# A graph network on one core: keep the rows' state in SBUF, fold the node work into the attention pass, and change the order of the blocks

## The chip, the core and the metric

The program runs on one core of one Trainium2 chip. The metric is the device time of one execution in microseconds, from three runs. The engines named below are PE (TensorE, matrix multiply; PEld is its weight load), DVE (VectorE), ACT (ScalarE), POOL (GpSimd, which here issues all gathers and scatters) and SP (SyncE, which here issues most plain DMAs).

## The reference, cut to what matters

There are 6250 nodes with 48 features and 200000 edges from `src` to `dst`; each edge has 40 attributes. Four graph layers follow each other. The first holds nearly everything that the change touches:

```python
h = _ln(h + agg / tot[:, None], gn, bn)          # agg, tot: gated sums over edges
logm = jnp.log(jnp.clip(node_mult, 1.0, None))
for i in range(4):
    Q = _ln(h @ Wq[i], gq[i], bq[i]);  K = _ln(h @ Wk[i], gk[i], bk[i])
    qi = Q[src];  kj = K[dst]
    score = (qi * kj).sum(-1) + 0.1 * (edge_attr * qi[:, :40]).sum(-1) + logm[dst]
    es = jnp.exp(jnp.minimum(score - segment_max(score, src)[src], 20.0))
    alpha = es / (segment_sum(es, src)[src] + 1e-10)
    aggi = segment_sum(alpha[:, None] * (h[dst] @ Wm[i]), src)
    z = jnp.concatenate([h, aggi], axis=-1) @ Wu[i]
    h = _ln(h + jnp.where(z > 0, z, 0.01 * z), go[i], bo[i])
```

The second layer is two plain neighbour sums, the third (`gated`) is a gated sum with a division by the same `tot`, the fourth is a normalised neighbour sum.

## The kernel before, in words

**Rows and blocks.** The nodes are padded to 6272, which is 49 blocks of 128. `build_grid` sorts the edges by source node into a grid: every node as a source gets a *row*, and the rows are ordered by how many edges do not fit the regular part. A row has 49 regular slots (one per block of destination nodes) and `WS[b]` overflow slots. `WS` falls from 28 in block 0 over 24, 17, 16, 15 and so on to 4 in block 48; it sums to 502. `grid.nat` holds, for every row, the node that it belongs to, so rows are in one order and nodes in another.

**first_sums** (line 1007) walks the 49 row blocks. It gathers each row's own element vector (`ei`, line 1060, from the table `tails`), picks destination rows from `table0` by one-hot matmuls (`pick_rows`), gathers those of the overflow slots one slot at a time (`tr_o`, line 1076), scatters lists for a later layer (line 1084), keeps the edge logit of the third layer in SBUF (`g.logit`), and scatters the block's sums by an indirect DMA into `agg0` in node order (`put_rows`, line 1197, called at the end of the block).

**node1** (line 1527) reads `agg0` back and normalises all 49 blocks at once.

**Four attention layers.** Each has three stages. The *qk* stage multiplies all nodes' `h` by Wq and Wk (`product`), normalises both (`norm`) with instructions over all 49 blocks, and writes `table_k` (K and h) and `table_q` to DRAM in node order (lines 1552 and 1553). `attend` (line 1205) first reads the whole `table_k` back and splits it into three bf16 parts (`load_table`, `exact_parts`, lines 981 to 990). Then, block after block in the order 0 to 48, it loads the one-hot rows `hot_t` and the attributes `at`, gathers the rows' queries (`q`, line 1222) and the overflow keys (`kh`, line 1225, one indirect DMA per overflow slot), picks the 49 regular slots by 147 matmuls (line 1002, copied out by ACT at line 1003), computes scores in three pieces (lines 1231 to 1233, the third piece being the overflow slots), the softmax (lines 1234 to 1240), a tree of adds (line 1193), and scatters the block's sum into `agg` (line 1199). The *up* stage (line 1556) reads `agg` back, multiplies by Wu, and updates `h`, again with instructions over all 49 blocks.

**gated_sums** (line 1251) has the same shape as `attend` with 48 wide rows and one product per slot; a later instruction multiplies its result by the reciprocal of `tot`.

**What sets the order.** Tiles of a pool rotate: `kh` in `attend` and `xe` in `gated_sums` have two buffers, so a block's gathers and its picks wait until the block two before it has been summed. A scheduler orders the instructions of each engine when the program is built; on the chip each engine then runs its list strictly in that order, and waits on semaphores. Gathers, scatters of sums and `q` share POOL's one list.

Of the kernel before, what the change touches and what calls it, by code (L numbers as in the profile page):

```python
# [18 lines left out]
F32 = mybir.dt.float32  # L19
BF = mybir.dt.bfloat16  # L20
# [479 lines left out]
T0 = H + 2 * G + 2  # L500

# [505 lines left out]
def first_sums(ctx: ExitStack, tc: tile.TileContext, g, keep, dram, table0, tails, agg):  # L1007
# [27 lines left out]
    g.logit = keep.tile([P, NB * NB + WO[NB]], F32, name="logit")  # L1035
# [18 lines left out]
    def overflow(b):  # L1054
# [4 lines left out]
        ei = sp.tile([P, 2 * G], F32, name="ei")  # L1059
# [52 lines left out]
    recs = load(0, spans, g.grid)  # L1112
    hrs = heads_to_rows(0, recs)
    others, ei = overflow(0)
    for b in range(NB):
        T = NB + WS[b]
        bs = g.bias[:, g.col[b] : g.col[b] + T]
# [4 lines left out]
        def add(t0, n, rec, tr):  # L1122
# [12 lines left out]
            nc.vector.tensor_mul(pr[:, :n], tr[:, :n, H : H + 2 * G], ei[:, None, :].to_broadcast([P, n, 2 * G]))  # L1135
# [3 lines left out]
            nc.vector.tensor_mul(g.logit[:, g.col[b] + t0 : g.col[b] + t0 + n], lg[:, :n, 1], rec[:, :, CW])  # L1139
# [23 lines left out]
        for i, (s0, n) in enumerate(spans):  # L1163
# [9 lines left out]
            if i == 1 and b + 1 < NB:  # L1173
                ahead = load(b + 1, spans, g.grid)
        if b + 1 < NB:
            hrs = heads_to_rows(b + 1, ahead)
# [3 lines left out]
        sm = sp.tile([P, H + 1], F32, name="sm")  # L1180
        add_up(nc, acc, PC, sm[:, :H])
        nc.vector.reduce_sum(sm[:, H:], ac[:, : len(done)].rearrange("p i o -> p o i"), AX.X)
        put_rows(tc, agg, g.nat, b, sm, "agg0")
        if b + 1 < NB:
            recs = ahead
            others, ei = overflow(b + 1)
# [18 lines left out]
def attend(ctx: ExitStack, tc: tile.TileContext, g, table_k, table_q, agg, name):  # L1205
# [3 lines left out]
    with tc.tile_pool(name=f"{name}_l", bufs=1) as lp:  # L1209
        parts = load_table(nc, lp, one, table_k, 2 * H, f"{name}_k")  # L1210
    sp = ctx.enter_context(tc.tile_pool(name=f"{name}_e", bufs=2))
    pp = ctx.enter_context(tc.tile_pool(name=f"{name}_ps", bufs=6, space=PSUM))
    TM = NB + WS[0]
    for b in range(NB):
        T, W = NB + WS[b], WS[b]
        hot = sp.tile([P, NQ // 4], I32, name="hot_t")
# [4 lines left out]
        q = sp.tile([P, H], F32, name="q")  # L1221
        nc.gpsimd.indirect_dma_start(out=q, out_offset=None, in_=table_q, in_offset=rows(g.nat, b))  # L1222
        kh = sp.tile([P, TM, 2 * H], F32, name="kh")
        for w in range(W):
            nc.gpsimd.indirect_dma_start(out=kh[:, NB + w], out_offset=None, in_=table_k,  # L1225
                                         in_offset=rows(g.idx, WO[b] + w))
# [466 lines left out]
```

## Time and profile before

The three runs took 15986.23 us in the median (15978.01 to 16000.76). The profiled execution took 15998.33 us by the device's time, and its span in the profile is 15996.5 us.

The span, cut by stage (busy us of each engine inside each window, all from the trace):

| stage | window, us | length | PE | DVE | ACT | POOL |
|---|---|---|---|---|---|---|
| build_grid and first nodes' work | 0 to 4488 | 4488 | 1922.83 | 2242.59 | 1277.35 | 2057.03 |
| first_sums | 4488 to 7237 | 2749 | 898.31 | 1321.60 | 1142.16 | 1185.58 |
| attend, layer 1 | 8683 to 9798 | 1115 | 484.62 | 803.64 | 257.48 | 778.36 |
| up 1 and qk 2 | 9798 to 9976 | 178 | 65.54 | 75.48 | 35.02 | 0.49 |
| attend, layer 2 | 9976 to 11105 | 1129 | 479.28 | 803.89 | 256.12 | 790.53 |
| up 2 and qk 3 | 11105 to 11283 | 178 | 65.54 | 75.48 | 35.25 | 0.54 |
| attend, layer 3 | 11283 to 12396 | 1113 | 474.63 | 803.52 | 256.19 | 780.06 |
| up 3 | 12396 to 12463 | 67 | 31.43 | 28.55 | 13.17 | 0.23 |
| second layer | 12463 to 14108 | 1645 | 719.28 | 348.14 | 172.66 | 987.98 |
| gated | 14108 to 15151 | 1043 | 285.46 | 476.05 | 117.07 | 711.47 |
| fourth layer | 15151 to 15996 | 845 | 340.05 | 203.31 | 74.97 | 495.98 |

To read it: an engine's busy time counts its instructions alone. POOL's list has a gap of about 0.30 us before each indirect DMA that the busy time leaves out. Where no engine is near the length of its window, the stage is a chain of waits; a wait is laid to the instruction that released it. The window of layer 0 and the stretches around it belong to the prediction below.

### The profile page before, as it was taken

Reading aid. Unit: us, or ns where it says so; the run is one execution under the profiler, and the core shown is the slowest. Engines: PE = TensorE matmul, PEld = TensorE weight load, DVE = VectorE, ACT = ScalarE, POOL = GpSimd, SP = SyncE. Lnnn points to the kernel's source line nnn. Section 1 sums busy time; section 2 is a strip of 40 time slices with the busy share of each in tenths; the row PEclk is TensorE's granted clock in tenths of the full one; section 3 lists DMA queues with packets and bytes.
Section 4 is the critical chain, followed back from the end, with each engine's and each line's share of the span. In section 5 each row is a group of like instructions: output and inputs, shape, how many; then the busy total and the mean of one; then the engine's idle time right before and its main releaser. Section 6 shows DMA issues by size and latency. Waiting matters only on the chain. (4 is left out here: it accounts for less than half of the span.)

```text
span 15996.5 us, 185891 instructions
## 1 busy us (share of the span) xinstructions
PE 6350.0 (40%) x69181; PEld 5257.0 (33%) x69181; DVE 8133.3 (51%) x15302; ACT 3955.4 (25%) x9383; POOL 8573.7 (54%) x7381
## 2 busy tenths in 40 slices
PE   1255444444412333332443444345344344532234
PEld 1234333333312222332343343344234333322233
DVE  8544444444424445554685686577578212134522
ACT  0133333333323344451222122122122101011100
POOL 0445555555444444433773773675577466666566
PEclk9955655556555556665665666666566566556566
DMA  8632222222145556663343343333334333233432
GB/s 299 202 117 85 54 57 55 56 55 56 49 137 166 183 190 209 216 232 82 108 128 76 105 125 88 96 116 95 97 112 123 66 67 69 66 90 116 119 79 57
DMA packets 1247387, 1798.32 MB, mean 112 GB/s; under 512 B 845706, under 2 KB 965998, under 8 KB 1188741
## 3 DMA queue, kind: packets, MB, share of 16 engines
q1 hardware_dynamic: 875810, 1059.45, 22.2%
q0 software_dynamic: 241632, 351.07, 10.2%
q10 hardware_dynamic: 129024, 375.81, 6.1%
q8 instruction: 543, 8.90, 0.2%
q14 instruction: 378, 3.10, 0.1%
HBM read 1220.28 MB, written 572.63 MB: 112 GB/s over the span
## 5 line engine op out<-in xcount | busy, mean ns | idle before, releaser
L1002 PEld LDWEIGHTS <-hot_t 128*128 128x128 fp8e4 x36015 | 2034.8, 117 | 3728.8 <-issue 3712.4
L1002 PE MATMUL pick_ps<-att_k_b,hot_t 128*128 128x96 bf16 x28812 | 1921.6, 242 | 2775.6 <-ACT kh L1003 1800.2
L1225 POOL DMA_INDIRECT kh<-table_k,idx_g x2008 | 2523.4, 1257 | 857.6 <-issue 547.8
L970 POOL DMA_INDIRECT grid<-rec,sloti x1666 | 1930.8, 1159 | 1863.8 <-DVE lf L684 1034.4
L1003 ACT COPY kh<-pick_ps 128x480 f32<-128x480 f32 (+1 forms) x1960 | 965.6, 568 | 3172.2 <-DVE sm L1195 1086.9
L1314 PE MATMUL h_ps<-x_parts,am 128*128 128x144 bf16 (+1 forms) x7203 | 856.6, 269 | 1185.8 <-issue 981.8
L1306 POOL DMA_INDIRECT xe<-table_c,lt x980 | 987.7, 1008 | 580.5 <-issue 277.3
L1231 DVE SCALAR_TENSOR_TENSOR kh<-at,kh 128x1000 f32<-128x1000 f32 (+9 forms) x588 | 575.1, 978 | 1167.2 <-DMA kh<-table_k,idx_g 437.7
L1314 PEld LDWEIGHTS <-am 128*128 128x128 fp8e4 x7203 | 632.4, 116 | 1384.5 <-issue 1380.6
L966 PE MATMUL pg<-w,hid 97*128 97x96 f32 x3332 | 693.1, 363 | 872.8 <-ACT hid L963 778.1
L966 PEld LDWEIGHTS pg<-w,hid 97*128 97x128 f32 x3332 | 603.6, 262 | 1144.9 <-ACT hid L963 886.3
L1311 DVE TENSOR_TENSOR h_hot<-ld,h_lanes 128x1280 bf16<-128x1280 bf16 x147 | 218.5, 1490 | 1348.0 <-remote 1109.8
L1002 PE MATMUL pick_ps<-table_b,hot_b 128*128 128x114 bf16 x7203 | 643.4, 257 | 573.4 <-issue 481.4
L900 ACT ACTIVATE junk<-dup_ps,less 128x128 bf16<-128x128 f32 x1666 | 588.7, 365 | 759.6 <-PE dup_ps L897 475.4
L1002 PEld LDWEIGHTS <-hot_b 128*128 128x128 bf16 x7203 | 549.8, 123 | 657.4 <-issue 657.1
L1222 POOL DMA_INDIRECT q<-table_q,nat x196 | 219.4, 1119 | 1004.1 <-DVE att_k_b L984 696.8
L967 DVE TENSOR_TENSOR rec<-pg,cut 128x384 f32<-128x384 f32 (+1 forms) x441 | 235.9, 535 | 996.7 <-remote 643.5
L1076 POOL DMA_INDIRECT tr_o<-table,idx_g x502 | 497.9, 992 | 421.7 <-DVE acc L1193 199.7
L1268 POOL DMA_INDIRECT xe<-table_g,idx_g x502 | 605.4, 1206 | 218.5 <-issue 145.7
L963 ACT ACTIVATE hid<-ph,w1b 96x512 f32<-96x512 f32 (+1 forms) x441 | 290.1, 658 | 1686.2 <-remote 1010.4
L1193 DVE TENSOR_TENSOR kh<-kh 128x96 f32<-128x96 f32 (+16 forms) x980 | 705.6, 720 | 0.4
L1168 PE MATMUL dt_ps<-f_identb,hot_b 128*128 128x128 bf16 x2401 | 279.5, 272 | 1011.2 <-DVE hot_b L1157 664.8
(408 smaller groups left out, 16014.9 us busy)
## 6 DMA issues: line engine op xcount, KB each, us to landing
hot_t<-hot SPq DMA_DIRECT2D x245, 784.0 KB
grid<-zero ACTq DMA_DIRECT2D x150, 1127.0 KB
recs<-grid SPq DMA_DIRECT2D x348, 483.0 KB
am<-adj SPq DMA_DIRECT2D x48, 2352.0 KB
hr<-heads_g SPq DMA_DIRECT2D x147, 448.0 KB
low<-lows SPq DMA_DIRECT2D x49, 1088.0 KB
gate_g<-g ACTq DMA_DIRECT2D x156, 336.0 KB
attr_g<-at ACTq DMA_DIRECT2D x156, 280.0 KB
```

Of the source, the lines that this page charges most:

```text
L900: nc.scalar.activation(junk, ps[:, t], AF.Sign, bias=less13[:, way : way + 1], accum_out=dup[:, t0 + t : t0 + t + 1])
L966: nc.tensor.matmul(pg[:, k], ht[:, k * P : (k + 1) * P], w2, start=True, stop=True)
L970: i = nc.gpsimd.indirect_dma_start(out=g.grid, out_offset=rows(sloti, t), in_=rec[:, t, :], in_offset=None, bounds_check=SLOTS - 1, oob_is ...
L1002: nc.tensor.matmul(ps[:, d], hot(db0 + d0 + d), parts[:, db0 + d0 + d, k], start=(k == 0), stop=(k == 2))
L1003: nc.scalar.copy(dst[:, d0 : d0 + m], ps[:, :m])
L1076: nc.gpsimd.indirect_dma_start(out=tr[:, w], out_offset=None, in_=table0, in_offset=rows(g.idx, WO[b] + w))
L1193: nc.vector.tensor_add(t[:, :k], t[:, :k], t[:, n - k : n])
L1225: nc.gpsimd.indirect_dma_start(out=kh[:, NB + w], out_offset=None, in_=table_k, in_offset=rows(g.idx, WO[b] + w))
L1231: nc.vector.scalar_tensor_tensor(k[:, :, :R], at[:, t0 : t0 + n], 0.1, k[:, :, :R], OP.mult, OP.add)
L1268: nc.gpsimd.indirect_dma_start(out=xe[:, NB + w], out_offset=None, in_=table, in_offset=rows(g.idx, WO[b] + w))
L1306: nc.gpsimd.indirect_dma_start(out=xe[:, t], out_offset=None, in_=table, in_offset=bass.IndirectOffsetOnAxis(ap=g.lt[:, d0 + d, t, 0:1], a ...
L1314: nc.tensor.matmul(ps[:, d], am[:, b, d * P : (d + 1) * P], parts[:, b].rearrange("p k f -> p (k f)"), start=(b == 0), stop=False)
```

## The change

The rows' state stays on chip in row order, and the node work is done in row order, seven blocks at a time.

- **Order of blocks.** All three row passes (`first_sums`, `attend`, `gated_sums`) visit the blocks as 0, 48, 1, 47, ..., 23, 25, 24 (`ORDER`), so that a block with many overflow slots alternates with one that has few. Position `pos` in this order is the index of all state kept on chip.
- **first_sums** gathers the row's own `h` along with `ei` (the rows of `tails` grow from 64 to 112 floats) and copies it to `h_rows`. It adds the block's sums straight into the SBUF tiles `agg0` and `tot_r`; the scatter of the sums is gone. The third layer's logit goes to DRAM (one small DMA per block from ACT's queue) instead of staying in SBUF.
- **node1 and the first qk** run over seven groups of seven positions. The normalisation (`scaled`) now takes its inverse square root by a shift and three Newton steps on DVE, where `norm` used ACT's square root.
- **attend** reads its query from SBUF (`q[:, pos]`) and has no gather of `q`. It writes its sum into `cat`, and after every seventh position calls `update`, which does for these seven blocks what *up* and the next layer's *qk* did for all: transposes, products, normalisations, then seven `put_rows` scatters into the next layer's `table_k`. `table_q` and `agg` are gone. The copies out of PSUM of these products move from DVE to ACT.
- **load of the table** goes through seven chunks of seven blocks, each split into parts as it arrives; the pool for `pick_ps` has 5 buffers where it had 6.
- **The last layer** scatters `h` to `h_nodes` and reads it back; `x` is read here and not before the four layers.
- **gated_sums** loads the logit, and multiplies the sum by the row's `tot_r` itself.

```diff
+ORDER = [b for i in range(NB // 2) for b in (i, NB - 1 - i)] + [NB // 2]
+GN = 7
...
-    g.logit = keep.tile([P, NB * NB + WO[NB]], F32, name="logit")
+    g.logit = dram.tile([NB, P, NB + OS], F32, name="logit")
...
-        ei = sp.tile([P, 2 * G], F32, name="ei")
+        ei = sp.tile([P, 2 * G + H], F32, name="ei")
...
-    for b in range(NB):
+    for pos, b in enumerate(ORDER):
+        after = ORDER[pos + 1] if pos + 1 < NB else None
         T = NB + WS[b]
+        nc.scalar.copy(h[:, pos], ei[:, 2 * G :])
+        lgt = sp.tile([P, NB + OS], F32, name="lgt")
...
-        sm = sp.tile([P, H + 1], F32, name="sm")
-        add_up(nc, acc, PC, sm[:, :H])
-        nc.vector.reduce_sum(sm[:, H:], ac[:, : len(done)].rearrange("p i o -> p o i"), AX.X)
-        put_rows(tc, agg, g.nat, b, sm, "agg0")
+        nc.scalar.dma_start(g.logit[b, :, :T], lgt[:, :T])
+        add_up(nc, acc, PC, agg[:, pos])
+        nc.vector.reduce_sum(tot[:, pos : pos + 1], ac[:, : len(done)].rearrange("p i o -> p o i"), AX.X)
...
-def attend(ctx: ExitStack, tc: tile.TileContext, g, table_k, table_q, agg, name):
+def attend(ctx: ExitStack, tc: tile.TileContext, g, table, q, name, update):
...
-    pp = ctx.enter_context(tc.tile_pool(name=f"{name}_ps", bufs=6, space=PSUM))
+    pp = ctx.enter_context(tc.tile_pool(name=f"{name}_ps", bufs=5, space=PSUM))
+    npp = ctx.enter_context(tc.tile_pool(name=f"{name}_nps", bufs=1, space=PSUM))
+    parts = one.tile([P, NB, 3, 2 * H], BF, name="k_parts")
+    rows_of = table.rearrange("(b p) f -> p b f", p=P)
+    for d0, n in chunks(NB, 7):
+        t = sp.tile([P, 7, 2 * H], F32, name="k_f")
+        nc.sync.dma_start(t[:, :n], rows_of[:, d0 : d0 + n])
+        exact_parts(nc, t[:, :n], [parts[:, d0 : d0 + n, k] for k in range(3)])
...
-        nc.gpsimd.indirect_dma_start(out=q, out_offset=None, in_=table_q, in_offset=rows(g.nat, b))
...
-            nc.vector.tensor_mul(k, k, q[:, None, :].to_broadcast([P, n, H]))
+            nc.vector.tensor_mul(k, k, q[:, pos : pos + 1].to_broadcast([P, n, H]))
...
-        nc.vector.tensor_scalar(sm, sm, den, None, OP.mult)
-        put_rows(tc, agg, g.nat, b, sm, f"{name}_agg")
+        nc.vector.tensor_scalar(cat[:, pos % GN, H:], sm, den, None, OP.mult)
+        if pos % GN == GN - 1 or pos == NB - 1:
+            update(np_, npp, pos // GN * GN, pos % GN + 1, cat)
...
+        lg = sp.tile([P, TM], F32, name="lg")
+        nc.sync.dma_start(lg[:, :T], g.logit[b, :, :T])
...
+    def scaled(np_, src, k):
...
+        yi = y.bitcast(I32)
+        nc.vector.tensor_scalar(yi, v.bitcast(I32), 1, None, OP.logical_shift_right)
+        nc.vector.tensor_scalar(yi, yi, -1.0, float(0x5F3759DF), OP.mult, OP.add)
+        nc.vector.tensor_scalar(v, v, -0.5, None, OP.mult)
+        for _ in range(3):
+            nc.vector.tensor_mul(s, y, y)
+            nc.vector.tensor_mul(s, s, v)
+            nc.vector.scalar_tensor_tensor(y, s, 1.5, y, OP.add, OP.mult)
+        nc.vector.tensor_mul(xc, xc, wide(y, H))
...
+    def ask(np_, pp, l, p0, n, table, q):
+        v = hr[:, p0 : p0 + n]
+        qk = np_.tile([P, n, 2 * H], F32, name=f"qk{n}")
...
+        times(np_, pp, v, H, n, wqk[:, l].rearrange("k t m -> k (t m)"), 2 * H, put)
+        xc = scaled(np_, qk.rearrange("p n (t f) -> p (n t) f", t=2), 2 * n).rearrange("p (n t) f -> p n t f", t=2)
+        nc.vector.tensor_mul(xc, xc, gqk[:, l : l + 1].to_broadcast([P, n, 2, H]))
+        nc.vector.tensor_add(q[:, p0 : p0 + n], xc[:, :, 0], each(bqk[:, l, 0], n))
+        kh = np_.tile([P, n, 2 * H], F32, name=f"khn{n}", bufs=2)
+        nc.vector.tensor_add(kh[:, :, :H], xc[:, :, 1], each(bqk[:, l, 1], n))
+        nc.scalar.copy(kh[:, :, H:], v)
+        for i in range(n):
+            put_rows(tc, table, grid.nat, ORDER[p0 + i], kh[:, i], f"table_k{l}")
...
+        def update(np_, pp, p0, n, cat):
+            v = hr[:, p0 : p0 + n]
+            nc.scalar.copy(cat[:, :n, :H], v)
+            zs = np_.tile([P, n, H], F32, name=f"zs{n}")
...
+            times(np_, pp, cat, 2 * H, n, wc[:, l], H, put)
             nc.vector.scalar_tensor_tensor(zs, zs, 0.01, zs, OP.mult, OP.max)
-            nc.vector.tensor_add(zs, zs, h)
-            norm(np_, h, zs, NB, each(go[:, l]), each(bo[:, l]))
+            nc.vector.tensor_add(zs, zs, v)
+            xc = scaled(np_, zs, n)
+            nc.vector.tensor_mul(xc, xc, each(go[:, l], n))
+            nc.vector.tensor_add(v, xc, each(bo[:, l], n))
+            if l + 1 < L:
+                ask(np_, pp, l + 1, p0, n, tables[l + 1], qs[(l + 1) % 2])
+            else:
+                for i in range(n):
+                    put_rows(tc, h_nodes, grid.nat, ORDER[p0 + i], hr[:, p0 + i], "h_nodes")
```

## The prediction

> **What bounds the kernel now.** I read first the busy shares, then the busy time by stage, then who waited for whom inside one attention pass, then the stretch between two passes in order of time.
>
> ```profile
> span 15996.5 us, 185891 instructions
> ...
> PE 6350.0 (40%) x69181; PEld 5257.0 (33%) x69181; DVE 8133.3 (51%) x15302; ACT 3955.4 (25%) x9383; POOL 8573.7 (54%) x7381
> ```
>
> No engine is near full over the whole span, so the answer lies in the stages. Columns below: window, its length, busy us (instructions) of each engine, granted clock, DMA share, GB/s. The windows are node1 with the first qk, the start and the rest of the first pass, and one stretch between passes:
>
> ```profile
> 7237.00:7386.00 149.00, 34.39 (x149) 28.34 (x148) 71.85 (x44) 26.16 (x23) 0.00 (x0) 0.50 0.24 50
> 7386.00:7500.00 114.00, 34.94 (x504) 29.47 (x505) 39.64 (x40) 17.74 (x35) 62.07 (x58) 0.59 0.47 106
> 7500.00:8505.00 1005.00, 448.17 (x6704) 416.82 (x6700) 764.12 (x1039) 238.66 (x555) 723.42 (x543) 0.65 0.40 114
> 8505.00:8683.00 178.00, 65.54 (x294) 57.48 (x294) 75.49 (x54) 35.39 (x37) 0.00 (x0) 0.50 0.19 41
> ```
>
> The reader is to see two kinds of stage. **Between passes** POOL does nothing and DVE is busy 75 of 178 us: a chain. **Inside a pass** DVE is busy 76%, POOL 72%, plus 0.30 us before each of its 543 DMAs (163 us): 886 of 1005. The waits inside the pass:
>
> ```profile
> DVE kh L1231 <- DMA kh<-table_k,idx_g: 103.3, 15, 16.6
> DVE kh L1231 <- DMA q<-table_q,nat: 80.7, 15, 10.6
> DVE kh L1231 <- issue: 29.1, 10, 8.6
> ...
> POOL kh L1225 <- ACT kh L1003: 62.9, 34, 3.7
> ```
>
> DVE lacks gathered rows for 184 us (the first two rows; the wait laid to `q` is the same wait for POOL's list), POOL lacks free buffers. Both are nearly full in turn. The chain between passes, in order of time:
>
> ```profile
> 8502.39 0.98 POOL L1199 DMA_INDIRECT agg<-sm,nat  x1 [7.80 <-DVE sm L1245]
> ...
> 8504.92 0.68 SPq L1559 DMA_DIRECT2D cat<-agg  x1
> ...
> 8641.23 0.37 SPq L1552 DMA_DIRECT2D table_k<-kh  x1
> 8652.01 0.68 SPq L990 DMA_DIRECT2D att_k_f<-table_k  x1
> ...
> 8683.18 0.99 POOL L1222 DMA_INDIRECT q<-table_q,nat  x1 [179.81 <-DVE att_k_b L984]
> ```
>
> From the last sum (8502) to the next pass's first gather (8683) pass 181 us: a re-read of 8.5, products, three normalisations with 2.61 us instructions over 2352 elements, a table write of 11 and a re-read of 12, then 19 of `exact_parts` one after another.
>
> **The change part by part.** I work against the span, 15996.5.
>
> *Stretch between passes, three times.* What remains on the path is the last group of seven blocks. Products: the same code took 5.5 us for two chunks (8513.4 to 8518.9), and 7 for the wider qk product (7272.9 to 7279.9). Vector work: 336-element instructions cost 0.49 (the 0.47 to 0.50 of line 1193's), 672-element ones 0.85, tiny ones 0.24 when each depends on the last (lines 1234, 1236, 1237 start 0.24 apart). Update: 8 x 0.49 + 14 x 0.24 + about 1 for ACT's square = 8. Ask: 5 x 0.85 + 2 x 0.49 + 14 x 0.24 + 1 = 10. Then seven scatters at 1.25 (0.95 + 0.30) and 2.5 to land (8502.39 to the release at 8504.85): 11. With handovers: 5.5 + 8 + 7 + 10 + 11 + 3 = **45**. The re-read in chunks (12 us of DMA, then parts of 0.6 to 0.8 us each) runs beside the first block's 28 gathers (35 us), which have no parts to wait for. So 181 becomes 45: **-408** in all. If that cover is gone, up to 20 per stretch come back.
>
> *node1 with the first qk.* The agg0 re-read (10) goes. Seven groups at 10 x 0.49 + 5 x 0.85 + 28 tiny at 0.16 (two groups interleave) = 13.6 of DVE make 95; a start at 7238, when the weights are in, and 21 for filling and the last scatters end at 7354 instead of 7386: **-30**.
>
> *End of the last layer.* 69 us from the last sum to the next normalisation become 5.5 + 8 + 11 + 11 (re-read) + 3 + 3: **-28**.
>
> *Order of blocks.* I cut the passes of before into pairs of neighbours and put time against their mean overflow count W: attend 30.8 us at W = 5, 42 to 45 at 10, 48.3 at 12, 54.7 at 14; first_sums 82, 110, 122, 138. Nearly straight lines, so mixing heavy with light gains little by itself. Reading each new pair off these points: attend's 47 later blocks 1016 us instead of 1002 (the two taken out of the list are now 28 and 4, not 28 and 24), and the first pair 87 instead of 114, since only 4 gathers follow the 28: **-13** per pass. gated is less straight (26 at W = 5, 42.5 at 10, 50 at 14, cheap light blocks lost): **+42**. first_sums: 0.
>
> *Inside the pass, POOL.* 49 gathers of `q` and 49 scatters of `agg` go, 49 scatters of the table come, all elsewhere in POOL's list (the built program puts the seven scatters three to four blocks after their update, so POOL doesn't stand at them). Per DMA 1.24 + 0.30: **-76** of POOL's list per pass at most; nothing, if DVE ends each pair.
>
> Here a rule speaks against the change: the Trainium skill (DMA: Bandwidth & Descriptors, "Rules for kernel authors") says to join small transfers, since under 64 KB one pays mostly overhead. One table write of 2.4 MB becomes 49 of 49 KB; by that page's fit (2.0 us plus bytes over 436e3, Anatomy of one DMA) 49 x 2.1 = 103 us, an estimate. The row is nearer: POOL is held 1.54 each, 76 us, and only the last seven end on the path. I take the row.
>
> *Inside the pass, DVE.* Each update adds 13.6 to 16, seven make 100 per pass (45 in the last, which has no ask). In the built program's list these instructions stand one by one between those of the next blocks, so their handovers to PE and ACT have cover, and some fill the 184 us of waits for gathers. Bounds: all hidden, 0; none, +100. I take half, **+50**.
>
> A second rule: the Trainium skill (GPSIMD Engine Reference, "Specifications") says that POOL's SBUF port is shared with VectorE, and that VectorE instructions with two SBUF inputs contend. The trace shows it in gated:
>
> ```profile
> 14652.05 3.10 DVE L1271 TENSOR_TENSOR gt<-gt,logit 128x2832 f32<-128x2832 f32 x1
> 14652.14 4.05 POOL L1199 DMA_INDIRECT agg_g<-sm,nat  x1 [7.58 <-DVE xe L1193]
> ...
> 14664.76 0.95 POOL L1268 DMA_INDIRECT xe<-table_g,idx_g  x1 [0.30 <-issue]
> ```
>
> By the rule taken whole, the two-input part of an update (60 of 100 us) would stop POOL for 60. By the rows, attend's 600 DMAs last 0.30 longer than 0.95 on average: 180 us of delay for 804 of DVE, so 100 more cost POOL 22. I take 22. Net of POOL: 76 - 22 = 54, of which some 60% count: -33, together with the DVE's +50 and the order's -13 about **+4**, less the last pass's missing ask and a shorter first wait; rounded, a pass goes from 1116 to **1095**: **-84** for four.
>
> *first_sums.* The scatter `agg` leaves POOL's list, where it stood behind the gathers' wait: 1.30 x 49 = 64; not every block is at POOL's mercy, so **-45** (ends -64 and 0). The logit's DMA (0.33 on ACT's queue) waits for the block's last logit; behind it stand copies that wait for the next loads anyway: 0, at worst 3 x 49. The tails' write of `h` goes out where SP stands idle for 90 us: 0.
>
> Sum: -408 - 30 - 28 - 84 + 42 - 45 = -553, less one 2.6 us product at the end: **15440** for the span. The median lies 10 below the span: **15430**.
>
> **The rivals.**
> - *Forecast: the serial stretches go, the pass stays as long.* 15200 to 15680. Chance 0.56.
> - *Both engines pack.* With `q` gone and gathers evened out, DVE's 904 us end the pass with 70 for its start: 975 to 1040, so 14950 to 15210, say 15080. For it: light blocks of before ran DVE at 88% (356 of 405 us). Against it: straight lines above. 0.20.
> - *Update added in full.* POOL's gain is void, DVE's 100 us come on top: 87 + 1016 + 100 = 1203 per pass, +348 for four; -408 - 30 - 28 - 45 + 42 - 3 + 348 = -124: 15860 in the median. 0.18.
> - *Slower: PE starves under the gathers.* While POOL gathers without pause, PE gets an instruction only every 1.4 us:
>
> ```profile
> 7441.64 0.24 PE L1002 MATMUL pick_ps<-att_k_b,hot_t 128*128 128x96 bf16 x1 [2.56 <-issue]
> ```
>
> An update and its ask need 42 matmuls with their weight loads; at 2.8 us a pair that is 118 us in the worst place, with DVE's list standing behind it. From 20 us per update (28 of them, 560) the gain is gone; at 30 the time is 16270. For it: 57 us of such idle time in the first 114. Against it: only 90 us in the other 1005. 0.06.
>
> **How the numbers follow.** Faster by over 0.2% (what a measurement of this kernel can tell from no change): the first three, 0.93 after rounding; within 0.2%: 0.01; slower: 0.06. The range holds the first case, more than half of the second, and nearly half of the third: 15030 to 15820.
>
> **What would show it.** Right: POOL's idle gap between passes falls from 180 to about 45; passes near 1095 with DVE near 900 busy; no `q` waits; gated 20 to 60 longer; first_sums near 2700. Wrong: a gap above 80 (the chunked load is on the path), passes under 1040 or over 1200, PE idle by issue well above 150 us in a pass, or first_sums shorter by over 100, which would mean that mixing pays where I read a straight line.

## The result, and the profile after

The changed kernel takes 15783.94 us in the median of four runs (15763.21 to 15806.52), beside 15993.49 us for the kernel before on the same chip: ratio 0.987, 95% interval 0.9853 to 0.9887. It is 210 us faster, where 556 were forecast. Its profiled execution took 15781.22 us, with a span of 15779.4.

The head of the page of the changed kernel, its span and its busy times:

```profile
span 15779.4 us, 186887 instructions
...
PE 6265.4 (40%) x69181; PEld 5146.0 (33%) x69181; DVE 8179.8 (52%) x16550; ACT 4043.8 (26%) x9678; POOL 8088.2 (51%) x7185
```

Against the kernel before, POOL does 486 us less work, DVE only 46 more. By busy times alone that looks like a gain of more than 210. So I cut both traces at the same events: the first gather of a pass, each block's sum on DVE, each write of `adj`. All in us; the forecast's terms are regrouped to these cuts.

| stage | before | after | difference | forecast |
|---|---|---|---|---|
| up to the first write of `adj` | 4600.6 | 4583.7 | -17 | 0 |
| first_sums, first to last write of `adj` | 2614.0 | 2539.3 | -75 | -45 |
| from there to the first gather of attention | 173.2 | 134.0 | -39 | -30 |
| first block of the first pass, and three times last sum to next first sum | 104.7 + 861.0 | 91.4 + 371.6 | -503 | -516 |
| four passes, each from first sum to last sum | 4039.6 | 4454.5 | **+415** | **+24** |
| last sum to the second layer's first gather | 110.6 | 70.2 | -40 | -28 |
| second layer | 1605.0 | 1607.5 | +3 | 0 |
| gated, first gather to last scatter | 1039.4 | 1084.9 | +46 | +42 |
| last layer | 848.4 | 842.3 | -6 | -3 |
| sum | | | -217 | -556 |

All stages but one came out near the forecast. The passes took 1129.7, 1127.5, 1130.1 and 1067.2 us, where the kernel before took 1009.4, 1005.4, 1020.2 and 1004.6. From here on "a pass" means this: first sum to last sum, 48 blocks. This cut has one fault: in the changed kernel the first two blocks of a pass end within 1.2 us of each other, in the kernel before 33 us apart. So where it matters a second figure stands beside it, the pass *with its start*, from the first gather to the last sum, which is what the forecast's 1095 means: 1111 to 1126 us before, and 1221, 1213, 1217 and 1152 after.

The busy time by stretch of the changed kernel: window, length, busy us (instructions) of PE, PEld, DVE, ACT and POOL, granted clock, DMA share, GB/s. The first is a stretch between two passes with the first block, the second a pass:

```profile
8478.00:8602.00 124.00, 34.81 (x397) 30.33 (x398) 59.84 (x98) 26.16 (x49) 38.79 (x39) 0.56 0.41 104
8602.00:9729.00 1127.00, 521.68 (x7100) 457.91 (x7099) 826.36 (x1298) 284.55 (x638) 620.81 (x512) 0.66 0.35 104
```

The same two of the kernel before:

```profile
8502.00:8789.00 287.00, 94.16 (x678) 80.88 (x679) 107.63 (x88) 48.23 (x61) 56.41 (x57) 0.53 0.29 66
8789.00:9794.00 1005.00, 456.00 (x6819) 425.08 (x6818) 770.95 (x1044) 244.26 (x566) 721.95 (x543) 0.66 0.39 115
```

In the pass DVE has 55 us more to do and POOL 101 less, and the pass is 122 us longer. DVE falls from 77% busy to 73%, POOL from 72% to 55%. No engine became the bound; the engines stand waiting for each other more. Who waited for whom in that pass of the changed kernel (total us, times, longest):

```profile
POOL kh L1240 <- ACT kh L1009: 344.8, 24, 44.4
PE pick_ps L1008 <- issue: 216.8, 294, 7.0
...
DVE kh L1246 <- DMA kh<-table_k,idx_g: 142.5, 18, 17.8
...
PE pt L1574 <- DVE cat L1260: 116.5, 11, 26.8
```

POOL's wait for a free `kh` buffer has grown from 71 us to 345, in 24 pieces. By itself that doesn't point to the order of the blocks: with the old order put back (e1 below) the same row of the second pass still has 295 us. The kernel before, then e1:

```profile
POOL kh L1225 <- ACT kh L1003: 71.4, 35, 5.6
```

```profile
POOL kh L1240 <- ACT kh L1009: 294.9, 28, 40.8
```

What the order does is seen at the second pair of the first pass (blocks 1 and 47). POOL's list in order of time, the last gather of this pair and the first of the next:

```profile
7384.83 0.96 POOL L1240 DMA_INDIRECT kh<-table_k,idx_g  x1 [0.30 <-issue]
7419.04 0.96 POOL L1240 DMA_INDIRECT kh<-table_k,idx_g  x1 [33.25 <-ACT kh L1009]
```

And DVE's in the same 34 us:

```profile
7392.02 1.20 DVE L1246 SCALAR_TENSOR_TENSOR kh<-at,kh 128x1000 f32<-128x1000 f32 x1 [25.83 <-ACT kh L1009]
...
7403.35 0.36 DVE L1246 SCALAR_TENSOR_TENSOR kh<-at,kh 128x200 f32<-128x200 f32 x1
...
7404.80 3.81 DVE L1255 TENSOR_TENSOR kh<-kh,sc 128x3504 f32<-128x3504 f32 x1
...
7417.99 0.31 DVE L1203 TENSOR_REDUCE sm<-kh 128x48 f32<-128x144 f32 x1
```

While POOL gathers (7349 to 7386), DVE has little to do; while DVE works (7392 to 7419), POOL stands. The light block's gathered piece (200 elements, 7403.35) stands in DVE's list ahead of the heavy block's weighting (3504 elements, 7404.80), so both blocks end together, both buffers come free together, and the next pair's gathers start only then. The pair takes 70 us, the sum of the two phases. In the kernel before, blocks 1 and 47 took 33 and 16. DVE's list has this order in the first four pairs (0 and 48 to 3 and 45); behind them the heavy block's weighting mostly stands first.

The first DVE row ends its wait with ACT's copy of the light block's picks, so PE has a part in it. While POOL gathers, a matmul comes mostly every 0.7 to 2.1 us (from 7362 to 7389):

```profile
7384.86 0.24 PE L1008 MATMUL pick_ps<-k_parts,hot_t 128*128 128x96 bf16 x1 [1.86 <-issue]
```

On chips where PE shows no such idle time this pair still takes 59 to 60 us (e10 below), so PE's part is some 10 of the 70.

### The profile page after: what moved, and what is told of

Its sections match the earlier page's. It is cut to its first block, busy times and chain, and to the rows that moved or that the text cites. A ratio compares the mean times of both kernels' runs of the same rounds, so it can differ in the third digit from the quotient of the medians.

```text
span 15779.4 us, 186887 instructions
## 1 busy us (share of the span) xinstructions
PE 6265.4 (40%) x69181; PEld 5146.0 (33%) x69181; DVE 8179.8 (52%) x16550; ACT 4043.8 (26%) x9678; POOL 8088.2 (51%) x7185
## 5 line engine op out<-in xcount | busy, mean ns | idle before, releaser
L1240 POOL DMA_INDIRECT kh<-table_k,idx_g x2008 | 2398.5, 1194 | 2032.7 <-ACT kh L1009 1348.3
L1008 PE MATMUL pick_ps<-k_parts,hot_t 128*128 128x96 bf16 x28812 | 1994.0, 241 | 1921.5 <-issue 874.4
L1246 DVE SCALAR_TENSOR_TENSOR kh<-at,kh 128x960 f32<-128x960 f32 (+13 forms) x588 | 572.7, 976 | 1108.1 <-DMA kh<-table_k,idx_g 668.1
L1286 POOL DMA_INDIRECT xe<-table_g,idx_g x502 | 650.8, 1296 | 419.3 <-ACT xe L1009 206.9
L1008 PE MATMUL pick_ps<-table_b,hot_b 128*128 128x114 bf16 x7203 | 608.8, 254 | 426.4 <-issue 386.6
L1201 DVE TENSOR_TENSOR kh<-kh 128x96 f32<-128x96 f32 (+15 forms) x980 | 703.0, 720 | 0.6
L891 DVE TENSOR_TENSOR pick<-look_ps,sb 128x441 f32<-128x441 f32 x588 | 342.9, 589 | 627.4 <-remote 423.4
```

The lines of the kernel that those rows point to most:

```text
L1008: nc.tensor.matmul(ps[:, d], hot(db0 + d0 + d), parts[:, db0 + d0 + d, k], start=(k == 0), stop=(k == 2))
L1201: nc.vector.tensor_add(t[:, :k], t[:, :k], t[:, n - k : n])
L1246: nc.vector.scalar_tensor_tensor(k[:, :, :R], at[:, t0 : t0 + n], 0.1, k[:, :, :R], OP.mult, OP.add)
L1286: nc.gpsimd.indirect_dma_start(out=xe[:, NB + w], out_offset=None, in_=table, in_offset=rows(g.idx, WO[b] + w))
```

## The experiments

Each kernel is the changed one with the edit shown. Five different chips served them, and on two of these (e5 to e8, e9 to e12) the kernel before took 14903 to 14911 us, on the others 15998 to 16055; numbers of one group are set only against the same group. e1, e11, e12, e17 and e18 ran four times, the others once. An update has two parts: the update of the nodes, and in every pass but the last the *ask* (function `ask`), which makes the next layer's queries and keys: products, normalisation, seven scatters into the table.

**The order and the updates, two by two.** e1 puts the order back; e2 and e3 call all updates after the pass.

```diff
-ORDER = [b for i in range(NB // 2) for b in (i, NB - 1 - i)] + [NB // 2]
+ORDER = list(range(NB))
```

```diff
-        if pos % GN == GN - 1 or pos == NB - 1:
-            update(np_, npp, pos // GN * GN, pos % GN + 1, cat)
+    for p0, n in chunks(NB, GN):
+        update(np_, npp, p0, n, cat)
```

> The changed kernel with its blocks in their old order (heaviest first) in every stage; all else as changed. I read each attention pass from its first block's sum to its last block's sum (48 blocks): 1010 us before, 1129 in the changed kernel (1067 in the last pass, which asks nothing). Theory A (the alternation is what lengthens the pass: a heavy block's gathers can't start until its buffer is free, and the light block beside them is too short to fill the time): 1020 to 1060, last pass 1000 to 1030. Theory B (the order is free; the seven updates are added in full): 1110 to 1140, last pass 1050 to 1080. In first_sums, from the first to the last write of adj: 2614 before, 2539 changed; if the alternation brought that, it goes back to about 2610, if the scatter that left did, it stays at 2540. Whole kernel by A: 15450 to 15650; by B: 15740 to 15880.

> The changed kernel with its seven updates of a pass called after the pass's last block, none inside it; order alternating as changed. All seven updates take the last group's sums, so the other six groups' sums are left out of the result. Read only: first sum to last sum of a pass. Theory A (alternation): 1050 to 1100, since the updates were mostly hidden. Theory B (updates in full): 1000 to 1030. By either the stretch after the pass is longer than in the changed kernel, about 100 to 150 us.

> Both at once: old order, and all seven updates after the pass (all take the last group's sums; the other six groups' sums are left out). First sum to last sum of a pass: both theories 970 to 1000, which is the 1010 of before less the part of 76 us that POOL saves by the q gathers and agg scatters that have gone. With e1 and e2 it makes a table of two by two: the order's cost with and without updates, the update's cost in either order.

Measured, passes 1 to 3 and the last:

| | updates after the pass | updates inside |
|---|---|---|
| old order | 978 to 980, 974 (e3) | 1086 to 1091, 987 (e1) |
| alternating | 1051 to 1056, 1054 (e2) | 1128 to 1130, 1067 (changed) |
| old order, with its start | 1087 to 1098, 1085 | 1197 to 1210, 1096 |
| alternating, with its start | 1137 to 1141, 1139 | 1213 to 1221, 1152 |

e14 and e15 are e2 and e3 on another chip, and the kernel before ran beside them as e13:

> As e2 (alternating order, updates after the pass; all take the last group's sums), under the conditions of e9 to e12. e9 and e10 give the alternation 35 us of a pass with asks and 50 without. Theory G (the heavy block's gathers wait for its buffer, by itself): 40 to 60 above e15. Theory T (the alternation costs by TensorE's slow instructions under two blocks' gathers in one go, of which there is none here): within 20 of e15.

> As e3 (old order, updates after the pass; all take the last group's sums), under the conditions of e9 to e12. Passes of 950 to 970, since e9's last pass, with updates and no asks, took 970; then an update without ask costs 0 to 20 per pass and the asks 75, as beside e1 and e3 (13 and 100).

> The kernel before, unaltered, so that its stages can be set against e9 to e12, which ran where TensorE shows no idle time by issue (152 to 318 us of it in each pass of e1 to e4, about 100 in before's own). Whole kernel near 14910. Pass from first sum to last sum: if that idle time lengthened the pass of before, 930 to 980 here instead of 1010; if it was beside the path, 990 to 1010. Stretch from last sum to next first sum 280 to 290 as before.

They did not land on the chip group that their expectations assume, so they only repeat the left column: 1050 to 1057 alternating, 978 to 988 in the old order (with the start 1135 to 1148 and 1086 to 1101). The kernel before had passes of 1029 to 1036 there, 20 more than in the first profile, so differences below some 20 us are not read.

What follows. Cut at the first sum, the alternation costs 75 us of a pass without updates, 80 of the last pass, and 40 beside the asks. About 24 us of each is the cut, since in the old order block 1 ends with block 0, ahead of it. With the start counted the alternation costs 43 to 54 us without updates, 56 in the last pass, and 11 to 20 beside the asks, which is no more than chips differ by. Most of the price without updates sits where the lists make two blocks end together: the start and the pairs 1 and 47 to 4 and 44 take 333 to 337 us in e2, and the same blocks 297 to 307 in e3.

An update that asks nothing (the last pass) costs next to nothing, 11 to 13 us in either order and by either cut. The asks cost 100 in the old order (1088 against 987) and 62 in the alternating one (1129 against 1067). Neither A nor B alone: A's price is there, B's is not the update's but the ask's, and the two overlap, so that together they cost less than one by one.

With its start e3's pass is 26 us below that of the kernel before (46 by e15 and e13, which shared a chip). That is what leaving POOL's `q` gathers and `agg` scatters out is worth; the chunked load and the fewer PSUM buffers are in this difference too. first_sums took 2569 in e1: of its 75 us, 45 come from the scatter that left and 30 from the alternation. The whole of e1 took 15704.75 us, ratio to before 0.9813 (0.9796 to 0.983): the old order is better than the new one in this kernel, but only by 79 us.

**TensorE at the transposes of an update (e4).**

```diff
-            times(np_, pp, cat, 2 * H, n, wc[:, l], H, put)
+            times(np_, pp, ready.to_broadcast([P, n, 2 * H]), 2 * H, n, wc[:, l], H, put)
+            nc.vector.tensor_add(zs, zs, cat[:, :n, H:])
```

> The changed kernel, but TensorE's transposes and products of an update read a tile of constants that is ready from the start, and the group's sums are added to their result on VectorE; so the product of the sums with the weights is left out (one vector instruction more per update). TensorE then never stands at a transpose waiting for a block's sums. Theory C (what an update costs is that TensorE stands at these transposes, with the next blocks' picks behind them in its list): the pass of 1129 falls by 40 to 90. Theories A and B: it stays within 15 of 1129.

1122, 1130, 1120 and 1079: theory C falls. The 116 us that PE stands at `cat` lie beside other waits.

**What an ask costs (e5 to e7, against e9).** e9 is e1 once more, as the row to set them against.

```diff
+        src = ready.to_broadcast([P, n, H]) if l else v
-        times(np_, pp, v, H, n, wqk[:, l].rearrange("k t m -> k (t m)"), 2 * H, put)
+        times(np_, pp, src, H, n, wqk[:, l].rearrange("k t m -> k (t m)"), 2 * H, put)
+        if l:
+            nc.vector.tensor_add(qk[:, :, :H], qk[:, :, :H], v)
```

> Old order, as e1, whose first three passes took 1088 us from first sum to last sum and whose last pass, without asks, took 987: an ask costs some 17 us. Here the products of an ask (layers after the first) read a tile of constants, and the nodes' values are added to their result on VectorE; so their product with the q and k weights is left out, and the ask's first vector instruction no longer waits for TensorE and ScalarE (e1: 22.8 us of such waits in a pass, one of 5.2 with the tail of a block behind it in VectorE's list). Theory P (these waits are what an ask costs): passes of 1020 to 1060. Theory V (its vector work is, set between the instructions of a block's tail, so that the block's buffer comes free later): 1065 to 1090. Theory S (its seven table scatters ahead of the next gathers): 1065 to 1090.

> Old order, as e1. The normalisation of an ask and its gain are left out after the first layer (two biased copies of the products stay): of 10 us of vector work 1 stays; products, copies and table scatters stay. Theory V: passes of 1000 to 1035. Theories P and S: 1060 to 1085.

> Old order, as e1. After the first layer no ask writes its rows; the first one writes its rows into all four tables instead, so later passes read the first layer's rows (node1 is longer by some 147 scatters). Theory S: passes of 1010 to 1045. Theories P and V: 1075 to 1090, since the last pass has as many scatters (of h_nodes) and took only 987.

> The kernel of e1 once more, as the row that this call's others are set against: in e5 to e8 the kernel before took 14903 us where it took 15998 beside e1, and first_sums 2130 where e1 took 2569, while the pass without asks took 972 where e1 took 987. If the price of an ask belongs to the kernel, the passes take 1075 to 1095 here too; if it belongs to the conditions under which e1 ran[...], 1000 to 1050.

e9's passes: 1048, 1039, 1046 and 970, so an ask's price depends on the conditions too (75 here, 100 beside e1). Against 1045: products ready 1011, no normalisation 991, no scatters 1004, with the last pass at 970 to 972 in all of them. Each of the three parts takes about half of the 75 or more with it (34, 54, 41), and together they would give 129. So they are not three separate prices. Links of one chain would look like this: products, vector work, scatters, and behind the scatters in POOL's list the next gathers. That it is this chain is argued from the program; no run shows it link by link. P, V and S are each half right.

e12 then tried to mend it: the vector work one block later than the products, pinned behind what is already in DVE's list.

```diff
-        nc.vector.reduce_sum(s, src, AX.X)
+        i = nc.vector.reduce_sum(s, src, AX.X)
+        if pin:
+            tc.keep_in_program_order(i)
...
+        if later and pos - later[0][0] == 1:
+            later.pop(0)[1](True)
```

> As e11, and the vector work of an ask is called one block later than its products and pinned behind that block's instructions on VectorE, so that it never stands waiting for TensorE and ScalarE. Nothing is left out. Theory P (the waits are the ask's price): passes 40 to 70 shorter than e9's. Theory V (its vector work in the tail of a block is): within 15 of e9's, as it still lies between a tail's instructions.

Passes of 1040 to 1045, last 974: what theory V expected, and not the 40 to 70 us of theory P; the whole took 14506.36 us (ratio 0.9726, 0.971 to 0.9743), level with e11. DVE's wait for the product was small (10 us a pass in e9) and stayed at 11. What e5 took away and e12 did not is PE's wait at the ask's transposes, with the next blocks' picks behind it. e9's pass, PE alone:

```profile
PE pt L1574 <- DVE h_rows L1631: 54.0, 6, 16.5
```

and e12's:

```profile
PE pt L1585 <- DVE h_rows L1649: 55.5, 6, 16.5
```

In e5 this row is gone, while PE's wait at the transposes of `cat` grew from 146 us to 314. That the row is e5's 34 us is argued; no run moves it alone.

**first_sums alone (e11).** The attention and gated stages run in the old order, first_sums alternates.

```diff
-    for pos, b in enumerate(ORDER):
-        after = ORDER[pos + 1] if pos + 1 < NB else None
+    for turn, b in enumerate(MIXED):
+        pos = b
+        after = MIXED[turn + 1] if turn + 1 < NB else None
```

> Old order in the attention passes and in gated_sums, alternating order in first_sums alone; all else as changed. first_sums 2539 against e1's 2569 beside the same kernel before, so 20 to 40 us below e1's order in the whole kernel, and about 110 below the changed kernel. If the alternation brings first_sums nothing, it is level with e9.

14502.35 us, ratio 0.9724 (0.9707 to 0.974), beside one run each of e9 (14534.88) and the changed kernel (e10, 14589.72). first_sums was level, 2124 against e9's 2126. Over all runs of these two chips it took 2113 to 2124 alternating (e8, e10, e11, e12: 2117 in the mean) and 2126 to 2133 in the old order (e5, e6, e7, e9: 2130), so the alternation is worth some 13 us here, where it brings 24 to 30 on the others. e11's 32 us over e9 lie in stages that its edit doesn't touch (12 of them ahead of first_sums), so nothing is read from them.

> The changed kernel once more, unaltered. Passes of 1129 and 1067 if they depend on the kernel alone; against e8 (1044 to 1062 with more buffers for heavy blocks) theory G expects passes of at least 1100 here, theory T within 20 of e8's.

e10's passes took 1076 to 1081 and 1020, which meets neither theory's figure: against e9's 1045 and 970 the alternation costs 33 and 50, or, with the start counted, 7 to 19 beside the asks and 27 in the last pass. In these passes PE has no idle time by issue at all. So the alternation costs something without any slow delivery of TensorE's instructions. With the delivery slow (217 us by issue in a pass of the changed kernel, 100 in the one before) it costs about the same beside the asks (11 to 20) and twice as much in the last pass (56). DVE's waits say the same: in the second pass it stands 66 us for picks in the changed kernel and 3 in e10.

**More buffers for the gathered rows (e8, e16).** The gathered rows get a tile of their own, in two sizes:

```diff
-        kh = sp.tile([P, TM, 2 * H], F32, name="kh")
+        kh = sp.tile([P, NB, 2 * H], F32, name="kh")
+        light = pos % 2
+        kg = sp.tile([P, 9 if light else OS, 2 * H], F32, name="kgl" if light else "kgh")
...
-        nc.vector.tensor_mul(kh[:, :T, H:], kh[:, :T, H:], sc[:, :T, None].to_broadcast([P, T, H]))
+        nc.vector.tensor_mul(kg[:, :W, H:], kg[:, :W, H:], sc[:, NB:T, None].to_broadcast([P, W, H]))
+        nc.vector.tensor_mul(kh[:, :, H:], kh[:, :, H:], sc[:, :NB, None].to_broadcast([P, NB, H]))
+        nc.vector.tensor_add(kh[:, :W, H:], kh[:, :W, H:], kg[:, :W, H:])
```

The edit is that of e16, with two buffers for light blocks; e8 has only one. The table chunk `k_f` has one buffer instead of two, and in e16 `cat` too.

> The changed kernel with its alternating order; the gathered rows have a tile of their own, two for heavy blocks and one for light ones, and their weighted values are added to the picked ones' ahead of the tree, so that a heavy block's gathers can start while the heavy block before is still at work. Theory G (the alternation costs because a heavy block's 12 to 28 gathers start only when the heavy buffer is free): passes of 1129 fall to 1060 or below, the last of 1067 below 1000. Theory T (it costs because two blocks' gathers then run without pause, and TensorE gets its instructions slowly meanwhile): it stays within 20 of 1129 or gets longer, with TensorE's idle time by issue above the 217 us per pass that it had.

> As e8, which gave the gathered rows of light blocks a single buffer and then stood waiting for these (270 us in its last pass): here heavy and light blocks have two each, so every block's gathers may start two blocks of its kind ahead. Against e10 (1078 with asks, 1020 without): theory G: below 1045 with asks and below 985 in the last pass, level with the old order's 1045 and 970 or better. Theory T: within 20 of e10's.

e8: passes of 1057, 1049, 1044, and 1062 in the last, against e10's 1078 and 1020: between the theories (with the start 1151 to 1172, no gain on e10's 1162 to 1169, and 1169 against 1104 in the last). The wait only moved. DVE in e8's last pass:

```profile
DVE kgl L1248 <- DMA kgl<-table_k,idx_g: 269.7, 21, 21.0
```

e16, with the second light buffer, ran on a chip of the slower group: passes of 929, 932, 931 and 893, and the whole kernel in 15168.3 us, beside 16047.09 for the kernel before. That is 198 us per pass below the changed kernel (174 in the last), in the same alternating order. Its start is longer, so with the start it is 144 to 156 (126 in the last). Its pass by busy time, in the columns of above:

```profile
8469.00:9401.00 932.00, 487.35 (x7100) 439.97 (x7100) 824.68 (x1394) 281.31 (x638) 678.38 (x479) 0.69 0.40 123
```

and its waits for gathered rows and for their buffers:

```profile
POOL kgl L1242 <- DVE den L1263: 30.4, 4, 11.9
DVE kgh L1248 <- DMA kgl<-table_k,idx_g: 28.7, 4, 13.3
...
DVE kgh L1248 <- DMA kgh<-table_k,idx_g: 18.5, 4, 7.6
...
POOL kgh L1242 <- DVE kh L1259: 17.3, 3, 6.5
POOL kgh L1242 <- DVE den L1263: 16.1, 4, 10.0
```

POOL's 345 us of waiting for buffers have become 64, DVE's 143 for rows 47; DVE is busy 88% of the pass. PE's idle time by issue fell as well, from 217 to 95 us a pass. So the buffers bound the changed kernel's passes. The asks cost less too (38 us, 931 against 893), so what e16 gains is not the alternation's price alone.

**The split tile in the old order (e17).** Two buffers of full size for `kg`, as `kh` had.

> Old order as e1, with the gathered rows in a tile of their own (two buffers, as before) whose weighted values are added to the picked ones' ahead of the tree, as in e8 and e16. In e16 the passes fell from 1129 to 931 and the last from 1067 to 893. Theory E (that came from the tile of its own, which comes free before the tree, in whatever order): passes here fall from e1's 1088 to 930 to 990. Theory G (it came from the heavy blocks' second buffer, which lets their gathers run beside a heavy and a light block): 1030 to 1080, last pass 940 to 985.

Both expectations missed: 1194, 1201, 1199 and 1197, the whole at ratio 1.0124 (1.0107 to 1.0141), slower than before. The list that the scheduler built says why. DVE in order of time:

```profile
9299.75 0.57 DVE L1247 SCALAR_TENSOR_TENSOR kg<-at,kg 128x400 f32<-128x400 f32 x1 [10.56 <-DMA kg<-table_k,idx_g]
...
9305.20 0.65 DVE L1258 TENSOR_TENSOR kh<-kh,kg 128x480 f32<-128x480 f32 x1
...
9326.21 0.57 DVE L1247 SCALAR_TENSOR_TENSOR kg<-at,kg 128x400 f32<-128x400 f32 x1 [10.26 <-DMA kg<-table_k,idx_g]
```

and POOL:

```profile
9306.12 3.21 POOL L1241 DMA_INDIRECT kg<-table_k,idx_g  x1 [9.36 <-DVE den L1262]
...
9322.10 0.95 POOL L1241 DMA_INDIRECT kg<-table_k,idx_g  x1 [0.30 <-issue]
```

DVE waits until 9299.75 for the rows of block k+1, and only behind that piece in its list does it weight and add up block k (9305.20), which frees the buffer that the gathers of block k+2 wait for (9306.12). Their last is issued at 9322.10, DVE goes on at 9326.21, and so on: a closed ring of 26 us per block, in which gathers and vector work alternate. It is the ring of the pairs again, one block at a time. By this reading, with two buffers the order of two instructions in DVE's list decides whether the gathers run ahead. e16 has the same order in its list, but its buffers are two per kind, so the next two blocks' gathers don't wait for block k. e17 shows that in the old order the tile of its own gains nothing (it costs 110 us a pass), so it is hardly what made e16 fast. What the old order would do with as many buffers, and what the list's order alone is worth, was not tried: that the alternation is better than the old order with such buffers is not shown.

**The stretch of e16 (e18).** The two casts of a table chunk go from ACT to DVE.

```diff
-        exact_parts(nc, t[:, :n], [parts[:, d0 : d0 + n, k] for k in range(3)])
+        hi, mid, lo = [parts[:, d0 : d0 + n, k] for k in range(3)]
+        nc.vector.tensor_copy(hi, t[:, :n])
+        nc.vector.tensor_sub(t[:, :n], t[:, :n], hi)
+        nc.vector.tensor_copy(mid, t[:, :n])
+        nc.vector.tensor_sub(lo, t[:, :n], mid)
```

> e16 with the two casts of each table chunk (the exact parts) on VectorE instead of ScalarE. In e16 the stretch from last sum to next first sum is 173 us where the changed kernel has 124: ScalarE's casts for the later chunks stand behind its copies of picks, and these behind TensorE, which is slow while 57 gathers run in one go. If ScalarE's list is what delays the first block, the stretch falls to 125 to 155 and the whole kernel by 60 to 150; if TensorE's slowness alone does, it stays at 165 to 180. Whole kernel near 15100, about 0.945 of the kernel before, either way below the changed kernel and below e1.

The stretches took 153, 158 and 174 us where e16 has 172 to 175, and the whole 15176.75 us: the forecast gain of 60 to 150 is not there, and one stretch of three didn't move. ACT's list is a part of it at most; why e16's stretch is 50 us longer than the changed kernel's stays open. But the version has its interval: 0.9493 of the kernel before (0.9474 to 0.9512), which beats both kernels.

## Why the prediction was wrong

**Stretches between passes: right.** The forecast of 45 us from last sum to next gather came out as 38. POOL at the first of them, last gather of the pass, first and last scatter of the table, first gather of the next pass:

```profile
8461.35 3.60 POOL L1240 DMA_INDIRECT kh<-table_k,idx_g  x1 [0.30 <-issue]
8505.72 1.00 POOL L1207 DMA_INDIRECT table_k<-khn,nat  x1 [40.78 <-issue]
...
8513.42 0.97 POOL L1207 DMA_INDIRECT table_k<-khn,nat  x1 [0.30 <-issue]
8516.40 0.99 POOL L1240 DMA_INDIRECT kh<-table_k,idx_g  x1 [2.00 <-issue]
```

Last sum at 8478, 28 us of products and vector work, seven scatters and their landing in 11: the row that was taken against the rule on small transfers held. The first block starts at once and the chunked re-read stays beside its gathers.

**POOL's saving inside the pass: right.** -33 forecast, -26 by e3 and -46 by e15. **first_sums' scatter: right** (-45, by e1); that the alternation brings this stage nothing was wrong by 13 to 30 us. **gated: right in size** (+42 forecast, +46), though by the traces only 26 of it is the order (1059 in e1, 1085 alternating); the other 20 are there in the old order too.

**The order of the blocks: a step that failed.** It was put at -13 per pass, 27 gained at the start and 14 lost in the later blocks, by reading each new pair off straight lines through pairs of neighbours. The gain at the start came (85 to 91 us, where e1 has 109 to 119). But the later blocks lose 75 to 80 us, or 40 beside the asks, so the order costs 43 to 56 or 11 to 20 per pass. The lines were drawn from pairs of nearly *equal* weight. There, each of the two buffers comes free one block after the other, and gathers of one block run beside the vector work of the other. In a pair of 24 and 5 gathers the light block's vector work is no cover for the heavy block's gathers, both blocks end together in DVE's list, and both buffers are handed over at once: the pair (1, 47) took 70 us, where 33 + 16 stood in the trace of before. A mean over two blocks can't show that, since it isn't weight that a buffer hands on but a moment.

**The updates: the other step that failed, by size.** +50 per pass was the middle between hidden and added in full, for updates with their asks. Measured 76 in the alternating order, 109 in the old one. The update itself is hidden (13, where half of 45 was allowed for); the ask isn't. The forecast counted its 10 us of vector work, half hidden, and its scatters by their time in POOL's list alone. Leaving out its products, its normalisation or its scatters takes 34, 54 or 41 us from a pass whose asks cost 75.

**The sum of a pass: not carried through.** Its terms gave +4 per pass, yet 1116 became 1095. The last pass's missing ask is worth 27 us once at half price, 7 per pass; the other 18 per pass, some 72 in all, stand for "a shorter first wait" that has no number, and the start's gain was already in the -13.

Together: four passes with their starts were to take 4380 us and took some 4800. Of these 420 us the sum has 72, POOL's saving 30, and the order and the updates 320. Since these two overlap, the order's part is 155 if the updates are counted first, and 250 if the order is.

**The rivals.** "Update added in full" gave 15860, near to the time. Its size holds for the asks in the old order (109 beside its 100), its account does not: without an ask the update costs 13 where it had 45, and POOL's saving is not void. "Both engines pack" had 975 to 1040 for a pass with its start. The changed kernel is far from it, and even with two buffers per kind e16's take 1064 to 1069, and 1026 only in the last, without asks. "PE starves" is there as a part: PE's idle time by issue did pass 150 us in a pass and three passes took over 1200, both of which the text named as signs of being wrong, but the alternation costs 7 to 27 us a pass, with its start, where PE has no such idle time.

## What to carry to other kernels

Pairing heavy and light work can even out the load only if the buffers let the heavy block's transfers start well before its turn; with two buffers taken in turn it made the transfers come in bursts here, and the engines alternate. Before a change of order is priced, write down for each transfer which instruction frees its buffer and what stands ahead of that instruction in its engine's list: the average load says nothing about it. And price work that is put inside a loop by the chain that it becomes part of, down to the queue it ends in, not by its busy time. When two kernels are cut at the same events, look at what falls outside the cut: here the first sum made the order look 24 us dearer per pass than it is.

## What the runs showed of the hardware that was not expected

The same program runs 7% faster on some chips. What differs most in the traces is idle time of PE by issue, in which it waits for nothing that the profile shows: 3048 us over the whole of e1, 2 us over e9, which is the same kernel. That this makes the difference is argued. It is not granted clock (0.632 and 0.640), and gated, with little of it in e1 (84 us), takes 1059 and 1055. The costliest PE group of first_sums in e1:

```profile
L1008 PE MATMUL pick_ps<-table_b,hot_b 128*128 128x114 bf16 x7203 | 632.2, 258 | 549.8 <-issue 477.0
```

and the same kernel in e9:

```profile
L1008 PE MATMUL pick_ps<-table_b,hot_b 128*128 128x114 bf16 x7203 | 556.9, 256 | 339.8 <-ACT tr L1009 339.6
```

In e9's passes PE shows none of it, in e1's 146 to 180 us each at the picks; first_sums took 2569 and 2126 us, the whole 15705 and 14535. What delivers the instructions more slowly on the one chip is not in the trace.

POOL's gathers grow longer the more they overlap with DVE: 1194 ns on average in the changed kernel, where they alternate with it, and some 1370 in e16, where they run beside it. In both, a gather that begins while DVE stands still takes 0.96 us, and one that begins beside a tensor_tensor of DVE 1.55 to 1.57 on average. The difference of the two means is 88 us per pass on 502 gathers, and e16 was faster all the same.
